# Splitting the first query tile's score product into two products of 64 queries

## The chip, the cores and the metric

The kernel runs on one core of one Trainium2 chip. The metric is the device time of one execution in microseconds (us). The kernel before took 626.9 us, the median of three runs (626.51 to 626.97).

## The reference, cut to what matters

The reference is two transformer layers on x of shape (2, 512, 256), all in fp32: attention, a gated feed-forward layer with dequantised weights, a linear attention, and a second feed-forward layer with looked-up weights. Only the first attention matters here. With 16 heads of 128 and a batch of 2 there are 32 heads to do, each over 512 positions:

```
q = rope(q); k = rope(k)
scale = 1.0 / np.sqrt(D_K)
attn = jnp.einsum('bihd,bjhd->bhij', q, k) * scale
causal = jnp.triu(jnp.ones((s, s), dtype=bool), k=1)
attn = jnp.where(causal[None, None], -jnp.inf, attn)
attn = jax.nn.softmax(attn, axis=-1)
o = jnp.einsum('bhij,bjhd->bihd', attn, v).reshape(b, s, N_HEADS * D_K)
```

Because of the causal mask, a tile of 128 queries needs only the keys up to its own end.

## The kernel before, in words

**Tiling.** The 512 queries of a head are four tiles of 128 (`it` = 0 to 3). Tile `it` is multiplied with the first 128 x (`it` + 1) keys, so its product has 128, 256, 384 or 512 columns. TensorE holds a tile of queries as its weights (128 x 128: the 128 numbers of a head by 128 queries) and streams the keys past them; the scores come out in PSUM with a query per partition and a key per column.

**Stages.** `sandwich_kernel` writes out one loop over 34 slots, `slot(i)`. Slot i computes the scores of head i, the projections of the queries and keys of head i + 1, the values and the output product of earlier heads, and the attention of head i - 1. After the heads come the first feed-forward layer (`ffn_hidden`, `ffn_out`), the linear attention and the second feed-forward layer (`silu_hidden`, `silu_out`); they don't use what the change touches.

**The scores of a head.** In slot i the products are issued in the order of tiles 3, 2, 0, 1. Tile 3 fills a PSUM bank `s3`; tiles 2 and 0 share a bank `s2` (columns 0 to 383 and 384 to 511); tile 1 has a bank `s1`. Each goes through `score_matmul`, line 908, and on to `scores`, where VectorE (DVE) scales and masks it, writes it to SBUF as `p` and takes the row's extreme in one reduction. ScalarE (ACT) then takes the exponentials (`exps`), and later scales them with the inverted sums. VectorE and DMAs turn the result (`turned_p`) for the product with the values in the next slot (`attended`).

```
s2 = bank("s")
score_matmul(i, 2, s2[:, :384])
score_matmul(i, 0, s2[:, 384:])
scores(i, 2, s2[:, :384])
exps(i, 3)
scores(i, 0, s2[:, 384:])
```

**What sets the order.** The kernel is written under a manual schedule: each engine runs its instructions in the order in which the code issues them. Two things depend on a model of time that the code itself keeps. `Times` and `Engine` hold an estimated clock for each engine; the helper `matmul` (its instruction is line 272) advances TensorE's clock `now` by a cost that goes by the columns streamed. First, `poll` resumes side chains (norms, linear attention) when `now` has come to their due time. Second, `Engine.fill` puts small lookup steps of VectorE (`select_in`, made into a queue `fills`) into gaps that the model sees on VectorE. VectorE, ScalarE and GpSimd (POOL) instructions are all issued by one helper and have line 181 in the profile; DMAs are issued from the SyncE queue (SP), line 163.

```
def matmul(out, lhsT, rhs, start, stop, **more):
    nc.tensor.matmul(out, lhsT=lhsT, rhs=rhs, start=start, stop=stop, **more)
    now[0] = max(now[0], times.start("PE", [out], [lhsT, rhs]))
    now[0] += (math.prod(rhs.shape[1:]) / 0.6 + 5) / 1e3
    times.add("PE", now[0], [out], [lhsT, rhs])
```

Of the kernel before, what the change touches and what calls it, by code (L numbers as in the profile page):

```python
# [17 lines left out]
ALU = mybir.AluOpType  # L18

P = 128  # L20
B = 2
S = 512
D = 256
NT = S // P
NK = D // P
NH = 16
# [6 lines left out]
HT = 2  # L33
TU = HT * P
NUNIT = B * NT // HT
TURNED = [P, 4, NK, HT, 32]
INTER = 688
NO = -(-INTER // P)
EPS = 1e-5
EPS_LIN = 1e-9  # L40
NEG = -1e30
WARM = 9
REST = INTER - (NO - 1) * P

# [144 lines left out]
def sandwich_kernel(  # L189
# [81 lines left out]
# [5 lines that stand above are left out]
# [10 lines left out]

    x0 = [const.tile([P, NT, D], F32, name=f"x0_{b}") for b in range(B)]
    cols_sb = const.tile([P, 3 * NH + 2 * NK], F32, name="cols_sb")
# [210 lines left out]
    with ExitStack() as at:  # L499
# [9 lines left out]
        def load(name, gg, part=None):  # L509

            if gg >= B * NG:
                return
# [30 lines left out]
        def warm_up(n):  # L543
# [5 lines left out]

        xTv = [ac.tile([P, NK, S], F32, name=f"xTv_{b}") for b in range(B)]  # L550


        xT0 = [
            ac.tile([P, NK, S] if b == 0 else [P, 4, NK, NT, 32], F32, name=f"xT0_{b}") for b in range(B)
        ]
# [259 lines left out]
        scale = 1.0 / math.sqrt(DK)  # L815
        NS = B * NH
        qT, kT, vs, pT, ps_p, yb = {}, {}, {}, {}, {}, {}
# [90 lines left out]

        def score_matmul(i, it, ps):
            n = (it + 1) * P  # L910
            matmul(ps, qT[i][:, it * P : n], kT[i][:, :n], True, True)

        def exps(i, it):
            p, mn = ps_p[i]
# [132 lines left out]
        def slot(i):  # L1047
# [29 lines left out]
            if now_in:  # L1077
                ps_p[i] = (
                    pr.tile([P, 1280], F32, tag="p", name="p"),
                    small.tile([P, NT], F32, tag="mn", name="mn"),  # L1080
                )
                sums[i] = small.tile([P, NT], F32, tag="sm", name="sm")
                s3 = bank("s")
                score_matmul(i, 3, s3)
                scores(i, 3, s3)
# [6 lines that stand above are left out]
                s1 = bank("t")  # L1092
                score_matmul(i, 1, s1[:, :256])
                scores(i, 1, s1[:, :256])
                exps(i, 2)
                exps(i, 0)
                exps(i, 1)
# [387 lines left out]
```

## Time and profile before

| | before |
|---|---|
| median of three runs | 626.9 us |
| the profiled execution's own time | 626.59 us |
| its span, first to last instruction | 624.8 us |
| granted TensorE clock | 1.00 |
| TensorE (PE) matmul busy | 618.3 us, 2502 instructions |
| TensorE weight load (PEld) busy | 462.5 us, 2502 instructions |
| VectorE (DVE) busy | 487.8 us, 1159 instructions |
| ScalarE (ACT) busy | 300.0 us, 659 instructions |
| GpSimd (POOL) busy | 276.7 us, 351 instructions |

All times in the profile come from one execution. A matmul in the code appears as weight loads (PEld) and matmuls (PE) of their own; the records of matmuls overlap, since one begins to stream before the one ahead of it has left the array, so busy time is not the sum of the mean times. A group's line gives line, engine, operation, output and inputs, their sizes and the count; then the busy time and the mean of one in ns; then the engine's idle time before them and what ended it. In the view of waits a line says who waited for whom, for how long in all, how often, and the longest. A timeline line is start, duration (both us), engine, line, operation, and how many were merged. The attention heads take the first 358 us or so of the span, some 11.2 us a head.

### The profile page before, as it was taken

Reading aid. Unit: us, or ns where it says so; the run is one execution under the profiler, and the core shown is the slowest. Engines: PE = TensorE matmul, PEld = TensorE weight load, DVE = VectorE, ACT = ScalarE, POOL = GpSimd, SP = SyncE. Lnnn points to the kernel's source line nnn. Section 1 sums busy time; section 2 is a strip of 40 time slices with the busy share of each in tenths; the row PEclk is TensorE's granted clock in tenths of the full one; section 3 lists DMA queues with packets and bytes.
Section 4 is the critical chain, followed back from the end, with each engine's and each line's share of the span. In section 5 each row is a group of like instructions: output and inputs, shape, how many; then the busy total and the mean of one; then the engine's idle time right before and its main releaser. Section 6 shows DMA issues by size and latency. Waiting matters only on the chain.

```text
span 624.8 us, 8228 instructions
## 1 busy us (share of the span) xinstructions
PE 618.3 (99%) x2502; PEld 462.5 (74%) x2502; DVE 487.8 (78%) x1159; ACT 300.0 (48%) x659; POOL 276.7 (44%) x351
## 2 busy tenths in 40 slices
PE   8999999999999999999999999999999999999996
PEld 7666666666666666666666688888888888888886
DVE  6979989877987989998988988869986372284853
ACT  5646666566565556656555651232313404416130
POOL 5354657355454465674667400350261151163341
PEclk9999999999999999999999999999999999999999
DMA  8467474575656646556462422211001001001000
GB/s 223 137 163 209 100 200 125 126 208 131 148 143 161 170 113 175 148 134 187 111 149 64 94 59 56 101 35 34 1 7 28 1 1 35 0 1 34 27 27 17
DMA packets 43580, 60.59 MB, mean 97 GB/s; under 512 B 5136, under 2 KB 31504, under 8 KB 43536
## 3 DMA queue, kind: packets, MB, share of 16 engines
q1 hardware_dynamic: 43536, 60.07, 37.1%
q8 instruction: 20, 0.33, 0.2%
q14 instruction: 24, 0.20, 0.1%
HBM read 28.33 MB, written 1.05 MB: 47 GB/s over the span
## 4 chain that ended last, share of the span: by engine, by line
PE 98%; issue 0%; DVE 0%; DMA 0%; POOL 0%; ACT 0%; POOLq 0%
PE ps_mm L272 39%; PE ps_o L272 22%; PE ps_s L272 22%; PE ps_t L272 15%; DMA x<-in_x 0%; DVE st L181 0%; POOLq L1481 0%; DVE mv L181 0%; POOL rstd L181 0%; ACT xT L181 0%; DVE x L181 0%; PE ps_t L278 0%; PE ps_s L278 0%; ACT wu L181 0%; POOL shift L181 0%
## 5 line engine op out<-in xcount | busy, mean ns | idle before, releaser
L181 DVE SCALAR_TENSOR_TENSOR rr<-ps_mm,cols_sb,sin_sb 64x512 f32<-64x512 f32 (+1 forms) x126 | 93.4, 741 | 4.3 <-PE ps_mm L272 1.3
L181 POOL TENSOR_TENSOR wg<-wg,scratch 128x752 f32<-128x752 f32 x30 | 53.7, 1791 | 91.0 <-DVE scratch L181 88.2
L272 PE MATMUL ps_mm<-xT,wg 128*128 128x256 f32 (+1 forms) x352 | 84.9, 379 | 0.0
L181 ACT ACTIVATE p<-p,mn 128x512 f32<-128x512 f32 (+3 forms) x128 | 70.6, 553 | 26.4 <-DVE mn L181 26.4
L272 PE MATMUL ps_s<-xT,wu 128*128 128x256 f32 x336 | 81.0, 379 | 0.0
L272 PE MATMUL ps_o<-wd,hT 128*128 128x256 f32 (+1 forms) x364 | 78.2, 372 | 0.0
L272 PE MATMUL ps_t<-pT,v 128*128 128x512 f32 (+3 forms) x256 | 74.2, 433 | 0.0
L272 PEld LDWEIGHTS ps_o<-wd,hT 128*128 128x128 f32 x364 | 67.4, 190 | 8.8
L272 PEld LDWEIGHTS ps_mm<-xT,wg 128*128 128x128 f32 (+1 forms) x352 | 66.4, 189 | 9.3 <-ACT ge L181 0.3
L272 PEld LDWEIGHTS ps_s<-xT,wu 128*128 128x128 f32 x336 | 63.8, 190 | 8.8
L272 PEld LDWEIGHTS ps_t<-pT,v 128*128 128x128 f32 x256 | 48.6, 190 | 27.9 <-issue 16.3
L181 DVE CUSTOM_DVE_ANT_0 p<-ps_s,mask 128x512 f32<-128x512 f32 (+2 forms) x96 | 46.0, 510 | 26.2 <-PE ps_s L272 25.9
L181 ACT ACTIVATE p<-p,rs 128x512 f32<-128x512 f32 (+3 forms) x128 | 61.4, 551 | 9.9 <-DVE rs L181 8.0
L272 PEld LDWEIGHTS ps_o<-wo,oT 128*128 128x128 f32 x256 | 48.6, 190 | 19.0 <-issue 12.9
L181 POOL TENSOR_TENSOR qT<-ra,rr 128x512 f32<-128x512 f32 x32 | 40.8, 1275 | 48.1 <-DVE rr L181 48.1
L272 PE MATMUL ps_s<-kT,qT 128*128 128x512 f32 (+2 forms) x192 | 60.8, 452 | 0.0
L272 PE MATMUL ps_o<-wo,oT 128*128 128x256 f32 x256 | 60.5, 379 | 0.0
L272 PE MATMUL ps_mm<-xT,wq 128*128 128x512 f32 (+1 forms) x128 | 58.6, 580 | 0.4 <-ACT xT L181 0.4
L272 PE MATMUL ps_mm<-xT,wk 128*128 128x512 f32 x124 | 58.3, 592 | 0.0
L272 PEld LDWEIGHTS ps_s<-kT,qT 128*128 128x128 f32 x192 | 36.1, 190 | 26.6 <-issue 15.7
L181 DVE STREAM_TRANSPOSE turned<-p 128x512 f32<-128x512 f32 (+3 forms) x128 | 54.1, 480 | 1.8 <-ACT p L181 0.9
L272 PE MATMUL ps_mm<-wv,xTv 128*128 128x256 f32 x232 | 54.9, 379 | 0.0
(147 smaller groups left out, 914.3 us busy)
## 6 DMA issues: line engine op xcount, KB each, us to landing
pT<-turned SPq DMA_DIRECT2D x128, 208.0 KB, 3.9
wo<-in_wo SPq DMA_DIRECT2D x17, 256.0 KB, 4.0
wv<-in_wv SPq DMA_DIRECT2D x16, 256.0 KB, 4.0
wq<-in_wq SPq DMA_DIRECT2D x15, 256.0 KB, 4.0
wk<-in_wk SPq DMA_DIRECT2D x15, 256.0 KB, 4.0
xT<-tr SPq DMA_DIRECT2D x44, 64.0 KB, 2.2
pk_g<-in_gate_p SPq DMA_DIRECT2D x4, 256.0 KB, 3.2
sc_g<-in_gate_s SPq DMA_DIRECT2D x8, 128.0 KB, 4.5
```

What stands on the lines that cost most here:

```text
L181: return write(*args, **more)
L272: nc.tensor.matmul(out, lhsT=lhsT, rhs=rhs, start=start, stop=stop, **more)
```

## The change

Tile 0 of a head, 128 queries by 128 keys, becomes two products: queries 0 to 63 into partitions 0 to 63 of the same PSUM columns, and queries 64 to 127 into partitions 64 to 127. Both are multiplied with the same 128 keys. The other three products are left as they are, and so is everything that reads the scores. In the built program the two new products are marked as tiles of 128 rows by 64 columns of TensorE's array, the one at column 0 and the other at column 64.

```diff
 P = 128
+HALF = P // 2
...
         def score_matmul(i, it, ps):
             n = (it + 1) * P
-            matmul(ps, qT[i][:, it * P : n], kT[i][:, :n], True, True)
+            if it:
+                matmul(ps, qT[i][:, it * P : n], kT[i][:, :n], True, True)
+                return
...
+            for q0 in (0, HALF):
+                matmul(
+                    ps[q0 : q0 + HALF],
+                    qT[i][:, q0 : q0 + HALF],
+                    kT[i][:, :n],
+                    True,
+                    True,
+                )
```

## The prediction

> **What bounds the kernel now.** I read the page's first and fourth part, then the waits of the two TensorE rows, then a table by stage, then the matmul groups by form, and at last the timeline of one head.
>
> ```profile
> span 624.8 us, 8228 instructions
> PE 618.3 (99%) x2502; PEld 462.5 (74%) x2502; DVE 487.8 (78%) x1159; ACT 300.0 (48%) x659; POOL 276.7 (44%) x351
> ...
> PE 98%; issue 0%; DVE 0%; DMA 0%; POOL 0%; ACT 0%; POOLq 0%
> ```
>
> TensorE is busy for 99% of the span and carries 98% of the chain that ended last. Busy alone proves little, since matmul records overlap; so the waits of TensorE and the stage that the change touches:
>
> ```profile
> PE ps_o L545 <- POOL mhalf L181: 1.0, 1, 1.0
> PE ps_mm L272 <- ACT xT L181: 0.4, 1, 0.4
> PE ps_t L272 <- ACT wu L181: 0.2, 1, 0.2
> ```
>
> ```profile
> core 0: us, PE busy (x) PEld busy (x) DVE busy (x) ACT busy (x) POOL busy (x), PEclk, DMA share, GB/s
> ...
> 15.00:358.00 343.00, 343.00 (x1227) 223.13 (x1227) 300.83 (x737) 210.47 (x501) 191.49 (x159) 1.00 0.56 146
> ```
>
> Three waits, 1.6 us in all, and all in the start-up. In the 343 us of the 32 heads TensorE is busy for all 343, while DVE has 42 us and ACT 133 us to spare, and the clock is granted in full (1.00). So TensorE's own stream sets the time of this stage: a nanosecond of array time added in a head is added to the end, and only array time taken away is a gain.
>
> The operation that is changed, by form, and one head of it (start, duration, engine, line, what, how often):
>
> ```profile
> L272 PE MATMUL ps_s<-kT,qT 128*128 128x128 f32 x64 | 12.3, 274 | 0.0
> ```
>
> ```profile
> L272 PEld LDWEIGHTS ps_s<-kT,qT 128*128 128x128 f32 x192 | 36.1, 190 | 26.6 <-issue 15.7 <-DVE hT L181 0.8 <-POOL kT L181 0.2
> ...
> L272 PEld LDWEIGHTS ps_mm<-xT,wg 128*112 128x112 f32 x16 | 2.8, 177 | 0.6
> ```
>
> ```profile
> 211.09 1.89 PE L272 MATMUL ps_s<-kT,qT 128*128 128x512 f32 x6
> 212.82 0.60 PE L272 MATMUL ps_t<-kT,qT 128*128 128x256 f32 x2
> 213.25 0.59 PE L272 MATMUL ps_mm<-xT,wq 128*128 128x512 f32 x1
> ```
>
> ```profile
> 212.60 0.19 PEld L272 LDWEIGHTS ps_s<-kT,qT 128*128 128x128 f32 x1
> 212.71 0.30 PEld L272 LDWEIGHTS ps_t<-kT,qT 128*128 128x128 f32 x2
> ```
>
> Three things are to be seen. First, each product in the code is two matmuls on the array: there are 32 heads and 64 of the 128x128 form, and six ps_s matmuls for the three products of 512, 384 and 128 keys. I call them passes. Second, the real cost of a pass is its distance to the next, not its 274 ns: from 211.09 to 212.82 the six passes stream 2 x (512 + 384 + 128) = 2,048 columns in 1.73 us, 0.845 ns a column, so a pass of 128 keys costs 0.108 us. The timeline of single loads agrees: the score loads at 212.60 and 212.71 and the next product at 212.82 are 0.11 us apart. I take 0.1095. Product 0 thus costs 2 x 0.1095 = 0.22 us in a head. Third, 274 - 109 = about 165 ns of each record lie behind the pass's streaming and are covered by the next pass, and the weight load of 190 ns lies under the pass before.
>
> **What the Trainium skill says.** "TensorE: Matmul & The Clock Gate", LDWEIGHTS: a load's time goes by the columns loaded, 0.83 ns each. The trace agrees: 112 columns take 177 ns and 128 take 190, 13 ns for 16. A load of 64 columns is then, by these two rows, about 137 ns.
> The same page, Part 3 (packing small matmuls): products in different column strips run at the same time (2.38 times faster for three of 32 columns), while matmuls start and end strictly in program order. Nothing in this trace shows either, because every matmul of before is 112 or 128 columns wide.
> "TensorEngine Tiling (Array Packing)", Key Properties: "Changing tiling mode (not just tile) drains the TensorE". No row shows that either, and no price is given. The tail of 165 ns is the bound that the trace has for one such drain.
>
> **The change, part by part.**
> The built program marks the two new products as tiles of 128 rows by 64 columns, at columns 0 and 64. They are in the narrow mode; all other matmuls are not. So a head switches into it once and out once.
>
> 1. Removed: 32 x 2 passes of 128 columns by 128 keys, 64 x 0.1095 = 7.0 us on the path.
> 2. Added: 32 x 2 products x 2 passes = 128 passes, each with 128 keys to stream past 64 columns. A pass is paid by its keys (the 0.845 ns a column held alike for 512, 384 and 128), not by the width of its weights, so each is 0.1095 us again where it runs alone: 14.0 us. All of it lies on the path, for there is no TensorE wait in the heads to hide it. Sum of 1 and 2: +7.0 us. The causal mask saves nothing: the first 64 queries are still multiplied with all 128 keys.
> 3. How much of it overlaps. The order is A first pass, A second, B first, B second, with starts in order. A's two passes share columns 0 to 63 and cannot run together, nor can B's. At the very most A's second and B's first overlap: three slots in place of four, +0.1095 x 32 = +3.5 us instead of +7.0. If a product's two passes did not exclude each other, two slots would do: +0. Bounds 0 and +7.0. I take +7.0: no row shows two matmuls of this type, two passes each, in parallel, and a pass has to be released while the pass ahead of it still streams.
> 4. Two mode switches a head. Lower bound 0; upper bound for each the tail, 0.165 us, and on top the load that could not be drawn ahead: some 0.137 us going in and 0.19 us coming out. 32 x (2 x 0.165) = 10.6 us, with the loads 32 x 0.657 = 21.0 us. I take 0 and keep the rest for the range; a short drain (a third of the tail at each switch, 3.5 us) together with the overlap of 3 comes to the same +7.0.
> 5. Weight loads: 128 of 64 columns in place of 64 of 128. Load time is equal in columns (128 x 64 = 64 x 128), and half as long a load hides easily under a 0.1095 us pass. 0. If they lost their cover it is the 21 us case of 4.
> 6. A new wait. The 384-key product, which had none, now waits for TensorE's own count, for the narrow products of the head before in that bank. Behind it on TensorE stand the rest of the head's products and the next projections; DVE's reductions wait for these. The count waited for was reached some 11 us before, so it is met on arrival. Such met waits already stand at the 512-key product of each head (on POOL) and the passes around it stay 0.43 us apart. 0; if a met wait cost an issue of 0.05 us, 1.6 us.
> 7. Moved: the helper that plans the order counts each product by its keys, so its clock is 0.22 us later per head, some 7 us at the end of the heads. In the built program TensorE, ACT, POOL and SP have the same order otherwise, transfers included, and the same counts. On DVE ten steps of the table lookups (pieces of 256 or 512 columns, 447 to 741 ns each) and one product of hidden units stand at other places, from the second half of the heads on. DVE is busy for 301 of 343 us there, and its reductions wait 25.9 us for ps_s; no TensorE matmul waited for it. Its cover is the spare 42 us; if ten such steps of about 0.5 us were all exposed it would be 5 us, and in the other direction at most the quarter of a us that separates the starts of two passes near 359 us beyond their streaming. 0.
> 8. The reduction of product 0 on DVE is third in its queue, behind those of 512 and 384 keys (687 and 556 ns), which begin before product 0 ends. 0.2 us later is not seen by it.
>
> Sum: -7.0 + 14.0 = +7.0. The profiled execution took 626.59 us, its span 624.8 plus 1.8 around it; 626.6 + 7.0 = 633.6. The median of the runs is 0.3 above the profiled one: 626.9 + 7.0 = **633.9 us**.
>
> **The rivals.**
> - *The halves overlap by one pass* (3): +3.5, 630.4 us. For it: the skill's measurements of column strips. Against it: a two-pass product between each pair, and the drains that would come on top.
> - *The switches drain the array* (4): between 626.9 + 3.5 + 10.6 = 641.0 with the overlap and 626.9 + 7.0 + 21.0 = 654.9 with nothing covered; 644.5 for two full tails and no overlap. For it: the skill's sentence. Against it: in columns the strips are independent, so the array might take the new width without emptying.
> - *Not slower: the halves run fully side by side.* One mechanism: the four passes go as two pairs, in 2 x 0.1095 us, from the point at which B's passes start within some 20 ns of A's and no drain is paid. Then the head costs what it did: 626.9 us. It cannot become faster by a measurable amount: the pair still streams 128 keys twice, 2 x 128 x 0.845 ns = 0.216, against the 0.219 paid now, a gain of at most 0.1 us in 32 heads.
> - *The change does not do what it says*, the array runs both products as full-width ones: then it is exactly two passes more, the forecast itself.
>
> **How the numbers follow.** Serial passes (or overlap and a short drain that come out alike), 632 to 636: 0.43. Overlap of a pass, no drain, 628.5 to 632: 0.22. Drains, 636 to 655: 0.26, about two thirds of it below 646. Side by side, 626 to 628.2: 0.06. Faster by some move of DVE steps that I don't see: 0.03. The range for 8 in 10 goes from 629.6 to 647. It leaves out the two last cases, the lowest edge of the overlap and the part of the drain case in which no load is covered, some 0.19. Beyond 0.2% (1.25 us, about what a measurement of this kernel can tell from no change): faster 0.03, same 0.05, slower 0.92.
>
> **What would show it.** In the trace of after, 128 score matmuls of 128 rows by 64 columns; from the first narrow pass to the ps_t product 0.44 us if serial, 0.33 with the overlap, 0.22 side by side. Drains show as a gap between the last 384-key pass and the first narrow one above 0.32 us, or between the last narrow pass and ps_t above 0.11, with loads that no longer lie under a pass. A head (now 11.2 us from one to the next) should be 0.22 us longer. If TensorE shows waits for DVE inside the heads, point 7 was wrong; if the head is longer by 0.5 us or more, point 4 was.

## The result, and the profile after

The changed kernel takes 637.0 us (median of four runs, 636.94 to 637.69) against 626.7 us for the kernel before on the same chip (four runs, 626.4 to 626.97): 1.0167 times the time, with a 95% interval of 1.0149 to 1.0184. It is slower by 10.3 us.

The lines of the page of the changed kernel that answer to those of before, from its first and fourth part. (One line more in the code has moved line 272 to 273 and 181 to 182.)

```profile
span 635.2 us, 8359 instructions
PE 628.3 (99%) x2566; PEld 458.3 (72%) x2566; DVE 487.3 (77%) x1159; ACT 301.5 (47%) x659; POOL 277.9 (44%) x351
...
PE 98%; issue 0%; DVE 0%; DMA 0%; POOL 0%; ACT 0%; POOLq 0%
```

Two more passes a head, 64 in all (2566 against 2502), and 10.0 us more of TensorE. The other engines' busy times moved by 1.5 us at most, weight loads apart (4.2 us less). What TensorE waited for, and the heads as a stage:

```profile
PE ps_o L546 <- POOL mhalf L182: 1.0, 1, 1.0
PE ps_t L273 <- ACT wu L182: 0.5, 1, 0.5
PE ps_mm L273 <- ACT xT L182: 0.4, 1, 0.4
```

```profile
15.00:368.00 353.00, 353.00 (x1288) 219.54 (x1287) 300.40 (x737) 211.68 (x501) 191.98 (x159) 1.00 0.55 141
```

No wait inside the heads, as before; TensorE fills the stage, and the stage is some 10 us longer. So the time is in TensorE's own sequence. The view of one tile (count; shortest, median and longest in ns; first and last start in us; forms, in the second line counted over every other matmul) shows how much, first before, then after:

```profile
L272 PE MATMUL ps_s<-kT,qT x192: 272/486/667, 14.9 to 360.4; 128*128 128x512 f32 x64, 128*128 128x384 f32 x64, 128*128 128x128 f32 x64
```

```profile
L273 PE MATMUL ps_s<-kT,qT x256: 272/404/649, 14.4 to 370.6; 128*64 128x128 f32 x64, 128*128 128x512 f32 x32, 128*128 128x384 f32 x32
```

From the first score matmul to the last it was 345.5 us and is 356.2. From one head's attention to the next, in the records of the trace, it was 11.203 us and is 11.547 for the heads in the middle, and the two shorter distances at the start (9.48 and 9.49 us before) grew by as much: 0.344 us a head, 11.0 us in 32 heads. The first score matmul starts 0.5 us earlier in this execution, which leaves about the 10.4 us by which the span grew.

Where in a head the 0.344 us lie is told by the groups by form and the timeline. First the ps_t passes before, then the groups of matmuls and of loads after:

```profile
L272 PE MATMUL ps_t<-kT,qT 128*128 128x256 f32 x64 | 19.1, 380 | 0.0
```

```profile
L273 PE MATMUL ps_t<-kT,qT 128*128 128x256 f32 x64 | 22.4, 431 | 0.0
L273 PE MATMUL ps_s<-kT,qT 128*64 128x128 f32 x128 | 14.1, 298 | 0.0
```

```profile
L273 PEld LDWEIGHTS ps_t<-kT,qT 128*128 128x128 f32 x64 | 9.5, 188 | 5.5 <-issue 5.3 <-DVE mn L182 0.2
L273 PEld LDWEIGHTS ps_s<-kT,qT 128*64 128x64 f32 x128 | 6.3, 134 | 17.4 <-issue 17.4
```

The 128 narrow passes are there. The ps_t passes behind them take 431 ns in the mean where they took 380, though nothing about them has changed. The timeline of one head, matmuls and loads:

```profile
240.66 1.18 PE L273 MATMUL ps_s<-kT,qT 128*128 128x384 f32 x6
241.77 0.70 PE L273 MATMUL ps_t<-kT,qT 128*128 128x256 f32 x2
```

```profile
241.40 0.20 PEld L273 LDWEIGHTS ps_s<-kT,qT 128*64 128x64 f32 x4 [0.55 <-issue]
241.77 0.30 PEld L273 LDWEIGHTS ps_t<-kT,qT 128*128 128x128 f32 x2 [0.17 <-issue]
```

Two gaps in the row of weight loads, 0.55 and 0.17 us, both put down to nothing that the profile shows ("issue"): one ahead of the first narrow load and one ahead of the first wide load after it. In the kernel before, each load ran under the pass ahead of its own here. The single records of that head, in ns from the span's start, which the timeline merges:

```
matmul  384 keys, second pass     starts 240987
load    64 columns                starts 241401, 241407
matmul  128 keys x 64 columns     starts 241402 (took 323), 241409 (323)
load    64 columns                starts 241456, 241462
matmul  128 keys x 64 columns     starts 241562 (272), 241569 (272)
load    128 columns (ps_t)        starts 241770
matmul  256 keys (ps_t)           starts 241772 (483)
load    128 columns (ps_t)        starts 241878
matmul  256 keys (ps_t)           starts 242092 (379)
```

Read from the top. Passes of 512 keys follow each other by 429 ns in this trace and passes of 128 keys by 109 in the kernel before, so a key takes 0.833 ns: the last wide pass streams its 384 keys in 320 ns, until 241307. The first narrow load comes only 94 ns later, with its matmul, so the load is not hidden: the matmul's record is 51 ns longer than that of the second pair (the second loads follow 55 ns after the first). Then both halves stream at once: two matmuls start 7 ns apart, and 160 ns later the next two. The last of these has streamed its 128 keys, 107 ns, by about 241676. Again 94 ns pass until the wide load, and it is paid in the open: the first ps_t record is 483 ns in place of 379, 104 more. So 128 keys x 2 passes cost about 2 x 107 ns, close to what they cost before, and the way in (94 + 51) and the way out (94 + 104) cost 343 ns, the 344 by which a head grew. The 32 heads repeat these distances to within 1 ns.

### The profile page after: what moved, and what is told of

It reads as the page before. It is cut to its first block, busy times and chain, and to the rows that moved or that the text cites. A ratio compares the mean times of both kernels' runs of the same rounds, so it can differ in the third digit from the quotient of the medians.

```text
span 635.2 us, 8359 instructions
## 1 busy us (share of the span) xinstructions
PE 628.3 (99%) x2566; PEld 458.3 (72%) x2566; DVE 487.3 (77%) x1159; ACT 301.5 (47%) x659; POOL 277.9 (44%) x351
## 4 chain that ended last, share of the span: by engine, by line
PE 98%; issue 0%; DVE 0%; DMA 0%; POOL 0%; ACT 0%; POOLq 0%
PE ps_mm L273 39%; PE ps_s L273 22%; PE ps_o L273 22%; PE ps_t L273 15%; DMA x<-in_x 0%; DVE st L182 0%; POOLq L1494 0%; DVE mv L182 0%; POOL rstd L182 0%; ACT xT L182 0%; DVE x L182 0%; PE ps_t L279 0%; PE ps_s L279 0%; ACT wu L182 0%; POOL shift L182 0%
## 5 line engine op out<-in xcount | busy, mean ns | idle before, releaser
L273 PE MATMUL ps_s<-kT,qT 128*64 128x128 f32 (+2 forms) x256 | 65.5, 419 | 0.0
L273 PEld LDWEIGHTS ps_s<-kT,qT 128*128 128x128 f32 (+1 forms) x256 | 30.3, 162 | 35.4 <-issue 25.9
```

## The experiments

The theory after the result: a switch between full-width products and halves costs an array that streams nothing for 94 ns and a weight load that isn't drawn ahead, 0.344 us for a pair of switches, and the halves run side by side at no cost. The rivals: the forecast's serial passes, a cost of each narrow product, and the VectorE steps that the planner's clock moved. Where `halves` stands in an edit, it is a helper that issues the two products of 64 queries and lets the clock count them as one (its matmul is line 279 there, that of `matmul` stays 272):

```diff
+    def halves(out, lhsT, rhs, start, stop, **more):
+        for q0 in (0, P // 2):
+            nc.tensor.matmul(
+                out[q0 : q0 + P // 2], lhsT=lhsT[:, q0 : q0 + P // 2], rhs=rhs, start=start, stop=stop, **more
+            )
+        now[0] = max(now[0], times.start("PE", [out], [lhsT, rhs]))
+        now[0] += (math.prod(rhs.shape[1:]) / 0.6 + 5) / 1e3
+        times.add("PE", now[0], [out], [lhsT, rhs])
```

All of them at a glance; a head's length is the median distance from one head's attention to the next in the records of the trace.

| kernel | median us | against before, 95% interval | a head, us |
|---|---|---|---|
| before | 626.2 to 626.7 | | 11.203 |
| changed kernel | 636.99 | 1.0167 (1.0149 to 1.0184) | 11.547 |
| halves_old_clock | 637.4 | 1.0173 (1.0158 to 1.0188) | 11.547 |
| tiles_0_1 | 637.09 | 1.0170 (1.0155 to 1.0185) | 11.547 |
| tiles_all | 636.84 | 1.0171 (1.0155 to 1.0186) | 11.547 |
| tiles_0_3 | 647.9 | 1.0343 (1.0326 to 1.0361) | 11.895 |
| again_both | 644.2 | 1.0283 (1.0268 to 1.0299) | 11.765 |
| by_keys | 633.12 | 1.0112 (1.0097 to 1.0127) | 11.427 |
| b_by_keys | 637.96 (one run) | | 11.559 |
| heads_narrow | 626.69 | 1.0003 (0.9994 to 1.0011) | 11.193 |
| causal_halves | 625.92 | 0.9994 (0.9985 to 1.0003) | 10.985 |
| causal_old_clock | 621.46 | 0.9923 (0.9907 to 0.9940) | 10.985 |

**The planner's clock put back.**

```diff
+            put = halves if it == 0 else matmul
+            put(ps, qT[i][:, it * P : n], kT[i][:, :n], True, True)
```

> The two products of 64 queries as in the changed kernel, but the helper's clock counts them as one product, so every VectorE step stands where it stood in the kernel before. Theory (two switches of column width per head, each with an idle array of about 0.094 us and a weight load that is no longer hidden; the halves stream side by side): 637.0 us, as the changed kernel, within 0.5. Rival (the moved VectorE steps carry part of the 10.3 us): 632 to 636.

637.4 us and the same 11.547 us a head. The moved VectorE steps carry nothing that these runs can tell.

**More narrow products behind the same two switches.** The condition becomes `it < 2` in one kernel and `True` in the other, so that four or eight narrow products stand in a row.

> Tile 1, which follows tile 0 directly, is computed in halves too: four narrow products, still one switch in and one out. Theory (switches cost, halves run side by side): 637.0, within 1. Rival (the forecast's serial passes): two more passes of 256 keys per head, 32 x 2 x 0.216 = 13.8 us more, 651.

> All four tiles of a head in halves: eight narrow products in a row, one switch in and one out. Theory: the switches are the whole cost and don't grow with what lies between them, 637.0 within 1. Rival (serial passes, 2,560 more keys to stream per head at 0.845 ns): 32 x 2.16 = 69 us more, about 706.

637.09 and 636.84 us: tile 1 adds nothing, and neither do all four tiles. Serial passes would have shown as 14 and 69 us. The ps_t passes, now narrow too and inside the narrow stretch, have their old mean again (kernel tiles_all):

```profile
L279 PE MATMUL ps_t<-kT,qT 128*64 128x256 f32 x128 | 19.3, 379 | 0.0
```

**Twice the switches.** The condition `it in (0, 3)` leaves the wide product of tile 2 between two narrow ones.

> Tile 3 in halves as well as tile 0, with the wide product of tile 2 between them: four switches per head in place of two. Theory: 11 us more than the changed kernel (32 x 0.343), 648. Rival that the cost is per narrow product and not per switch, and that narrow products stream serially: 32 x 2 x 0.429 = 27.5 us more for the passes, 664.

647.9 us, 10.9 more than the changed kernel; a head is 0.348 us longer. The second pair of switches costs what the first one does, though it encloses a product of 512 keys where the first encloses 128. It is the switch that is paid, not what is narrow.

**Twice the narrow work.** Both narrow products of tile 0 are issued a second time.

> The two narrow products of tile 0 are computed twice over (the same scores written again; work added). Switches as in the changed kernel. Theory (side by side): two more slots of 128 keys per head, 32 x 2 x 0.109 = 7.0 us more, 644. Rival (serial): four more passes, 14 us more, 651.

644.2 us, 7.2 more than the changed kernel, 0.218 us a head: the time of two passes of 0.109, not of four. And the repeated passes (line 925) show no load in the open, while the first ones (line 279) do:

```profile
L279 PE MATMUL ps_s<-kT,qT 128*64 128x128 f32 x128 | 14.0, 298 | 0.0
L925 PE MATMUL ps_s<-kT,qT 128*64 128x128 f32 x128 | 12.4, 273 | 0.0
```

**The same split without a switch.** Tile 0 as two products of 128 queries by 64 keys, at full width.

```diff
+            for k0 in (0, P // 2):
+                matmul(
+                    ps[:, k0 : k0 + P // 2], qT[i][:, :n], kT[i][:, k0 : k0 + P // 2], True, True
+                )
```

> Tile 0 split the other way: two products of all 128 queries with 64 keys each, full width, so no switch of width, and four passes of 64 keys. If a pass is never shorter than its weight load of 128 columns (0.107 us): 32 x 2 x 0.107 = 6.8 us more than before, 633.5. If a pass goes by its keys alone: 626.7. If the mere splitting in two products made the cost of the change: 637.

633.12 us, 6.6 more than before, 0.224 us a head. Four passes of 64 keys take as long as four weight loads of 128 columns; the records of the loads follow each other by 109 to 113 ns. Here a pass at full width is not shorter than its load. (In the next kernel passes of 64 keys with loads of 64 columns follow each other by 57 to 59 ns, so it is not a fixed cost of a pass.) So a split without a switch costs less than the 10.3 us, and it costs for another reason: each part loads all the columns anew, while the halves load half each.

**Which pass is which.** As the changed kernel, but the second half's product is cut in two of 64 keys each (line 916).

```diff
+            matmul(ps[: P // 2], qT[i][:, : P // 2], kT[i][:, :n], True, True)
+            for k0 in (0, P // 2):
+                nc.tensor.matmul(
+                    ps[P // 2 :, k0 : k0 + P // 2],
+                    lhsT=qT[i][:, P // 2 : P],
+                    rhs=kT[i][:, k0 : k0 + P // 2],
+                    start=True,
+                    stop=True,
+                )
```

> As the changed kernel, but the second half's product is two products of 64 keys, so that the records tell which pass is which by their length (one look). Theory (each half of the columns works through its own passes): time as the changed kernel, 637, and the first 64-key pass starts with the first 128-key pass, ahead of the second one that stands before it in the program. Rival (starts in the program's order, one after another across the halves): both 128-key passes start before any 64-key pass, some 0.1 us per head more, 640.

One run, 637.96 us, too few for a verdict on the time; the order of the passes is what it is for. The timeline of a head:

```profile
126.66 0.33 PE L916 MATMUL ps_s<-kT,qT 128*64 128x64 f32 x2
126.81 0.27 PE L272 MATMUL ps_s<-kT,qT 128*64 128x128 f32 x1
126.82 0.28 PE L916 MATMUL ps_s<-kT,qT 128*64 128x64 f32 x2
127.03 0.48 PE L272 MATMUL ps_t<-kT,qT 128*128 128x256 f32 x1
```

Two passes of line 916 start ahead of a 128-key pass of line 272, which belongs to a product that stands before theirs in the program; the first 128-key pass starts at 126.65, 8 ns ahead of the first of them. The order of the six passes is the same in all 32 heads. Each half of the columns works through its own passes as its own turn comes. This is how the two passes of a product, which share their columns, don't keep the other half from starting.

**No switch inside a head.** From head 2 to 29 the helper `matmul` issues every product in halves, projections, values, attention and output included.

```diff
-        nc.tensor.matmul(out, lhsT=lhsT, rhs=rhs, start=start, stop=stop, **more)
+        for q0 in (0, P // 2) if narrow[0] else (None,):
+            cs = slice(None) if q0 is None else slice(q0, q0 + P // 2)
+            nc.tensor.matmul(out[cs], lhsT=lhsT[:, cs], rhs=rhs, start=start, stop=stop, **more)
...
+            narrow[0] = 2 <= i < NS - 2
```

> Every product of heads 2 to 29 (projections, scores, values, attention, output) in two halves of 64 columns; twice the matmul instructions, two switches in the whole run. Theory: with no switch inside a head, the time of the kernel before, 626.7, within 1.5. Rival (a narrow product has a cost of its own, such as its issue or its weight load): 56 products more per head and over 0.02 us each would make 630 and above.

626.69 us, no difference from before, with 1,116 more matmuls on the page (about 40 passes a head, so 20 products and not the 56 of the expectation):

```profile
PE 618.3 (99%) x3618; PEld 433.8 (69%) x3618; DVE 488.0 (78%) x1159; ACT 300.0 (48%) x659; POOL 277.5 (44%) x351
```

So narrow products in pairs are free in all the shapes of these heads; only crossing between full width and halves is not. Nor is every change of width a crossing: in all these kernels four groups of 112-column passes stand among passes of 128 columns after the heads, and in the kernel before the passes of 256 keys follow each other there by 215 to 216 ns on the way in and out, as everywhere else. In the built program they are marked as tiles of 128 by 128; the halves are the only products with another mark.

**A use for it.** If halves are free and run on their own, each can stream only the keys that its 64 queries may see. `causal_halves` does so in heads 3 to 29. For tiles 0 and 1 the earlier queries sit in the upper half of the columns, with a mask to match and the halves put back in the output product, so that both halves of the array have equally much to stream. Four PSUM banks are held fixed through these heads. The scores that are no longer written are all under the mask.

```diff
+            at = HALF if it < 2 else 0
+            for q0, m in ((0, n - HALF), (HALF, n)):
+                to = slice((q0 + at) % P, (q0 + at) % P + HALF)
+                q = slice(it * P + q0, it * P + q0 + HALF)
+                nc.tensor.matmul(ps[to, :m], lhsT=qT[i][:, q], rhs=kT[i][:, :m], start=True, stop=True)
+            now[0] += ((n - HALF // 2) / 0.6 + 5) / 1e3
...
+                in1=mask_sw[:, 2 * P - n :] if is_causal(i) and it < 2 else mask[:, S - n :],
...
+                    swapped=is_causal(i) and t < 2,
```

> All products from head 2 on in halves, so that no switch lies inside a head, and in heads 3 to 29 each half of the columns streams only the keys that its 64 queries may see: 64 keys fewer for the earlier half of every tile. The earlier half sits at columns 0 to 63 for tiles 3 and 2 and at columns 64 to 127 for tiles 1 and 0, so that each half of the array streams 1,152 keys per head and pass in place of 1,280. Theory (halves work through their own passes independently): 27 heads x 2 passes x 128 keys x 0.845 ns = 5.8 us less than before, 620.9. Rival (a half waits for the other one at each product, so the longer one sets every product): no gain, 626.7.

625.92 us: no gain, the number of the rival, but not by its mechanism. Most heads took 10.985 us, 0.218 less than before, as the theory says. But the gain did not reach the end. Two stages after the heads, from 358 to 420 and 420 to 480 us of the span, in causal_halves:

```profile
358.00:420.00 62.00, 60.89 (x408) 46.20 (x403) 48.88 (x131) 13.38 (x24) 12.73 (x32) 1.00 0.17 49
420.00:480.00 60.00, 58.51 (x268) 50.24 (x267) 51.26 (x101) 20.90 (x37) 17.53 (x39) 1.00 0.10 23
```

TensorE is idle for 1.1 and 1.5 us where before it was never idle (62.00 of 62 and 60.00 of 60 us busy), and the longest of its new waits are for the hidden units on VectorE and the gate on ScalarE (in the causal kernels `matmul` is line 279 and the score products are line 925):

```profile
PE ps_s L279 <- DVE hT L182: 1.6, 2, 1.1
PE ps_mm L279 <- ACT ge L182: 0.7, 1, 0.7
```

The idle time is less than what these waits cost, since the record of a pass outlasts its streaming by some 163 ns (379 against 216 for 256 keys): from start to start, the passes after 358 us stand 4.6 us further apart in all than such passes usually do. The built order shows why VectorE could be late: with the shorter products on the clock, side chains of norms and linear attention are issued at other places between the hidden units on ScalarE, VectorE and GpSimd. The next kernel changes only that line of the clock.

```diff
-            now[0] += ((n - HALF // 2) / 0.6 + 5) / 1e3
+            now[0] += (n / 0.6 + 5) / 1e3
```

> causal_halves with one line other: the helper's clock counts a score product by all its keys, as in the kernel before, so that VectorE, ScalarE and GpSimd work in the order of the kernel before (two copies of a mask added). In causal_halves a head took 10.985 us in place of 11.203, and the lead of 4.6 us at the last head was lost between 410 and 560 us of the span, where the side chains were ordered otherwise. Theory (the order by the clock lost the lead): it is kept, 626.2 - 5.3 = about 621, at least below 623. Rival (what follows the heads is bound by VectorE, whatever the order): 625 to 626.

621.46 us, 0.9923 of before (0.9907 to 0.9940), 4.8 us faster. The waits of TensorE:

```profile
PE ps_o L552 <- POOL mhalf L182: 1.0, 1, 1.0
PE ps_t L279 <- ACT wu L182: 0.7, 1, 0.7
PE ps_mm L279 <- ACT xT L182: 0.4, 1, 0.4
PE ps_t L279 <- DMA pT<-turned: 0.3, 1, 0.3
```

They are those of the start-up and one of 0.3 us, and after the heads the passes stand only 0.2 us further apart than usual. So what was lost behind the heads was lost by the order. Of 27 x 0.218 = 5.9 us, 4.8 arrive. The records of the heads tell where the rest goes: two heads ahead of the 27 are together 0.45 us longer than before, the wait of 0.3 us among it, and four of the 27 take 11.043, 11.378, 11.139 and 11.194 us in place of 10.985, 0.8 us in all.

## Why the prediction was right in its direction and wrong in its mechanism

It said slower with 0.92, and 637.0 lies in its range. But the likeliest case, serial passes, did not happen: two of its terms were wrong, one by 7.0 us too much and one by 11.0 us too little. That they had opposite signs, and left the sum only 3.1 us short of the 637.0, is luck.

- **What bounds the kernel** held: TensorE's sequence sets the time of the heads, and what is added there arrives at the end.
- **Point 1**, 7.0 us removed, and the pass of 0.1095 us: held (again_both: 0.218 us for the time of two passes).
- **Points 2 and 3 failed**, "I take +7.0". The step argued that A's two passes share their columns, that starts follow the program, and that so at the very most one slot of four could be saved. The first is right. The second does not hold for passes, as b_by_keys shows: the other half starts at once, between the two passes of the first. The added streaming was about 7.0 us, and 1 and 2 cancel: 0, the lower bound that was given and not taken.
- **Point 4 failed**, "I take 0". It was bounded by 0 and 21.0 us and measured at 0.344 x 32 = 11.0. The tail of 165 ns was too much for the idle array (94 ns), and the records of 137 and 190 ns too much for the loads: what is paid in the open is 51 and 104 ns.
- **Point 5**, loads that stay hidden: held within a width, not across a switch.
- **Points 6 to 8**, the met wait, the moved VectorE steps, the later reduction: 0, as said, as far as these runs can tell. The starts around the new wait stay 0.43 us apart, halves_old_clock shows no gain from the old order, and TensorE waits for nothing in the heads.
- **The signs** that it named: both gaps of a drain were there, 0.415 us (above 0.32) and 0.203 (above 0.11). But a head that is 0.5 us longer was to show that point 4 was wrong, and it was wrong at 0.344: that sign counted on the 0.22 us of serial passes.
- **The rivals**: "side by side" had the streaming right and failed on "no drain is paid". "The switches drain the array" had the mechanism right, but was priced on top of passes that overlap by one or not at all, at 641.0 to 654.9. No rival put the two together: 626.7 + 0 + 11.0, less the 0.5 us of the start-up, is 637.2. Of the remaining two, "does not do what it says" is out, as the trace has the 128 narrow passes, and nothing became faster.

What stays open is what the array does in the 94 ns. The records show that neither load nor pass crosses a switch before the pass ahead has streamed and 94 ns have gone by; that the array empties in this time is what the Trainium skill says ("TensorEngine Tiling (Array Packing)", Key Properties), and fits, but no run here shows it.

## What to carry to other kernels

Before putting a product into a part of TensorE's columns, count the changes between full width and halves in the order of its instructions, not the products: here each pair cost 0.344 us, as much as streaming some 400 keys, whatever stood between. Put narrow products in a row, or a whole stage in halves. In these heads the halves themselves then cost nothing, and they are worth having where each can skip work of its own and both have equally much. And a gain on the bounding engine can be lost afterwards by a planner whose clock has moved: repeat it with the old order before giving it up.

## What was not expected of the hardware

- Passes in different halves of the columns don't wait for each other's place in the program: in b_by_keys two 64-key passes of a later product started 153 and 46 ns ahead of the second 128-key pass of the product before it. The Trainium skill, "TensorE: Matmul & The Clock Gate", Part 3, says that matmuls start and end in program order; taken pass by pass, the starts in these records show otherwise. Taken by products they agree, since the first passes of the three products do start in the program's order; the ends of matmuls are modelled in the profile and can't tell. The page's other statement, that column strips run at the same time, agrees (starts 7 ns apart).
- The Trainium skill, "TensorEngine Tiling (Array Packing)", Key Properties, sets a change of the tiling mode apart from a change of the tile alone, and the runs agree: changing from full width to halves costs (0.344 us a pair), and changing only the tile, from columns 0 to 63 to columns 64 to 127, does not (heads_narrow at 626.69 us).
- A weight load's record is longer than what it costs in the open: 134 ns against 51 for 64 columns, 188 ns against 104 for 128.
